# Layer 1 of a two-layer state-space kernel: 128 + 64 channels against three groups of 64 channels with two states per unit

## The chip, the core and the metric

The kernel runs on one core of a Trainium2 chip. A core has five engines that run side by side, each with its own instruction queue: TensorE (PE: matrix products into PSUM, with its weight loads shown apart as PEld), VectorE (DVE), ScalarE (ACT), GpSimd (POOL) and SyncE (SP, which here issues most DMAs). The metric is the device time of the whole kernel in microseconds, taken as the median of several runs; a profile gives one execution in detail, with the time of every instruction and the clock that TensorE was granted.

## What is computed

The input is a 64 x 64 picture with 96 channels (4096 tokens). Two layers follow one another, each with group norm ahead and a residual around it. Layer 0 is a scan in four directions, and the change does not touch it. Layer 1 is one forward scan over all 4096 tokens (192 inner channels, 16 states):

```python
xz = jnp.einsum('blc,ec->ble', u, W_in)
xs, z = jnp.split(xz, 2, axis=-1)
xc = silu(causal_conv(xs, conv_w, 3 taps) + conv_b)
dbc = jnp.einsum('bld,ed->ble', xc, W_x)          # dt (6), B (16), C (16)
delta = jax.nn.softplus(dt @ W_dt + b_dt)
dA = jnp.exp(delta[..., None] * A)
dBu = delta[..., None] * Bm[:, :, None, :] * xc[..., None]
h = dA_t * h + dBu_t                              # token after token
y = jnp.einsum('bdn,bn->bd', h, C_t)
out = ((y + xc * D) * silu(z)) @ W_out
```

All data are float32, except that B is split into three bfloat16 parts that add up to it, and is spread by a bfloat16 product.

## The kernel before

Layer 1 (class `Layer1`, line 709) works in 4 chunks of 1024 tokens (`CH`). In a chunk there are 24 *units*. A unit is one scan of a tile of 128 partitions x 1024 tokens, and its operations are spread over all engines:

- `load` (L895): a DMA brings the unit's rows of C from DRAM, each row repeated over partitions.
- `spread` (L909): PE multiplies a selection matrix `pick` with the split B (`parts`), two matmuls of 512 tokens, so that B of the unit's states stands in every partition of a PSUM tile `f`.
- `decay` (L901): ACT makes `dA` = exp(A dt).
- `scan` (L920): DVE multiplies `f` in place with `w` = dt u, and then scans `h` = dA h + f. The `f` pool has two buffers.
- `keep_last` (L929): ACT keeps the last column of `h` as the carry-in of the same unit in the next chunk.
- `times_c` (L933): POOL multiplies `C` in place with `h`.
- `fold` (L937): PE adds the result to `y` in PSUM.

The 192 channels are cut in 128 + 64. The first 16 units are the 16 states of the first 128 channels. In the last 8 units the two halves of the partitions hold two states of the other 64 channels, and `fold` adds the halves with a matrix `both` of 64 columns: the first 512 tokens go to partitions 0 to 63 of `y1`, the second 512 to partitions 64 to 127. A float32 matmul is recorded as two instructions, called *records* below; a bfloat16 one as one.

All front tiles (`u`, `sz`, `e`, `dt`, `w`) have 128 partitions x 1536 columns: 1024 columns for the 1024 tokens of the first 128 channels, and 512 columns whose partition halves are the two token halves of the other 64 channels. For the last 8 units this packed part of `dt` and `w` is copied by eight DMAs of 128 KB into `dt1` and `w1` (end of `front_dt`, L853), where both halves of the partitions hold all 1024 tokens. The first 16 units read `dt` and `w` themselves.

The order of each engine's instructions in layer 1 is the program's order (class `Ordered`). `run` (L1014) goes through all units; at step s it issues load(s+3), spread(s+1), keep_last(s-1), decay(s+2), scan(s), times_c(s-1), fold(s-2), and then one piece of `between` (L1000): the front of the next chunk and the back of the one before, cut by `yield` into pieces. The pieces are, in order: xn on ACT, three convolutions `pc` (`front_u`), in chunks 1 to 3 the back (`gate` of y1, and two pieces with the output product `po`), three products `pz` (`front_z`), silu on ACT with the first `pd`, the second `pd` with the DMA of C to DRAM (`front_dbl`), three `pv` (`front_v`), four pieces of softplus (exp, then `q` on ACT and `acc` on DVE, `front_dt`), one with the end of softplus and the copies, and two that split B (`front_b`). Products of these pieces share one PSUM buffer `misc`. For chunk 0 the front is run ahead of the first unit, in the order u, silu, dbl, b, v, dt, z.

`load_layer1` (L149) brings the weights at the very start of the program by seven DMAs on SP; the DMAs of x on SP stand behind them.

## Time and profile before

| what | us |
|---|---|
| median of 3 runs | 815.01 (811.65 to 816.62) |
| the profiled execution | 810.95 |
| its span, first to last instruction | 808.8 |
| layer 1: from its first xn to its first scan product | 300.3 to 355.25 |
| the four chunks (first product to first product) | 107.4, 116.5, 113.8, 90.0 |
| from the last scan's end to the end | 25.85 |
| busy over the span: PE, DVE, ACT, POOL | 633.6, 532.6, 325.2, 282.9 |
| mean granted TensorE clock | 0.808 |

Read it so: an engine's busy time says how much of the span it worked, and not that it set the end; "idle before" names what an engine waited for ahead of a group of instructions. The chunks are the part to look at, since each runs the same 24 units with a different amount of front and back work among them. DMA shares are means over 16 engines.

### The profile page before, as it was taken

Reading aid. Unit: us, or ns where it says so; the run is one execution under the profiler, and the core shown is the slowest. Engines: PE = TensorE matmul, PEld = TensorE weight load, DVE = VectorE, ACT = ScalarE, POOL = GpSimd, SP = SyncE. Lnnn points to the kernel's source line nnn. Section 1 sums busy time; section 2 is a strip of 40 time slices with the busy share of each in tenths; the row PEclk is TensorE's granted clock in tenths of the full one; section 3 lists DMA queues with packets and bytes.
Section 4 is the critical chain, followed back from the end, with each engine's and each line's share of the span. In section 5 each row is a group of like instructions: output and inputs, shape, how many; then the busy total and the mean of one; then the engine's idle time right before and its main releaser. Section 6 shows DMA issues by size and latency. Waiting matters only on the chain.

```text
span 808.8 us, 4869 instructions
## 1 busy us (share of the span) xinstructions
PE 633.6 (78%) x1497; PEld 238.4 (29%) x1497; DVE 532.6 (66%) x439; ACT 325.2 (40%) x458; POOL 282.9 (35%) x163
## 2 busy tenths in 40 slices
PE   1599999799999968549866699865699854796576
PEld 1344444343222222113221135321145320252115
DVE  2500359714975650188679977679987779989970
ACT  1211694513432222654663523664433662433200
POOL 9000000000000000206447954535954555856550
PEclk9699999989755586559888789896599985799955
DMA  6200170000000010046334723252634333554500
GB/s 150 78 1 0 57 199 0 0 1 19 0 10 10 21 38 0 3 114 198 100 111 110 201 105 118 83 159 54 193 118 140 115 106 96 191 152 152 148 9 24
DMA packets 29461, 68.49 MB, mean 85 GB/s; under 512 B 13008, under 2 KB 13420, under 8 KB 28978
## 3 DMA queue, kind: packets, MB, share of 16 engines
q1 hardware_dynamic: 26874, 65.91, 28.0%
q10 hardware_dynamic: 2552, 2.18, 1.0%
q8 instruction: 14, 0.23, 0.1%
q14 instruction: 21, 0.17, 0.1%
HBM read 60.36 MB, written 3.56 MB: 79 GB/s over the span
## 4 chain that ended last, share of the span: by engine, by line
PE 48%; DVE 28%; ACT 13%; issue 5%; DMA 2%; POOL 2%; SPq 1%; DVEq 0%; POOLq 0%; ACTq 0%
DVE h L695 13%; PE y L695 10%; PE pc L544 8%; PE po L695 5%; DVE f L695 4%; PE pc L695 4%; DVE acc L695 3%; PE pd L695 3%; PE f L695 3%; ACT dA L695 3%; PE pe L527 2%; DMA xt<-in_x 2%; PE pq L185 1%; PE pv L695 1%; PE pq L184 1%
## 5 line engine op out<-in xcount | busy, mean ns | idle before, releaser
L695 POOL TENSOR_TENSOR C<-C,h 128x1024 f32<-128x1024 f32 x96 | 234.9, 2453 | 177.7 <-DVE h L695 127.9
L695 DVE TENSOR_TENSOR_SCAN h<-dA,last,f 128x1024 f32<-128x1024 f32 x72 | 169.0, 2347 | 9.3
L695 DVE TENSOR_TENSOR f<-f,w 128x1024 f32<-128x1024 f32 x96 | 116.7, 1216 | 35.7 <-PE f L695 35.6
L695 PE MATMUL y<-C,ident 128*128 128x512 f32 x256 | 134.3, 648 | 0.1
L695 PE MATMUL f<-parts,pick 96*128 96x512 bf16 x192 | 69.9, 453 | 80.3 <-DVE h L695 79.8
L544 PE MATMUL pc<-pad,cw 96*128 96x512 f32 x288 | 127.2, 602 | 0.0
L695 ACT ACTIVATE dA<-dt,A 128x1024 f32<-128x1024 f32 x96 | 109.6, 1147 | 37.9 <-DVE h L695 37.4
L544 PEld LDWEIGHTS pc<-pad,cw 96*128 96x128 f32 x288 | 55.1, 192 | 70.6 <-issue 70.3
L695 PEld LDWEIGHTS y<-C,ident 128*128 128x128 f32 x256 | 53.4, 209 | 48.6 <-issue 39.1
L695 PE MATMUL y<-C,both 128*64 128x512 f32 x128 | 51.7, 902 | 16.5 <-POOL C L695 16.4
L695 PEld LDWEIGHTS <-pick 96*128 96x128 bf16 x192 | 14.0, 103 | 166.6 <-DVE h L695 126.7
L695 DVE TENSOR_TENSOR_SCAN h<-dA,f 128x1024 f32<-128x1024 f32 x24 | 54.9, 2287 | 2.9
L555 DVE TENSOR_SCALAR u<-u,d 128x512 f32<-128x512 f32 x16 | 8.3, 523 | 73.1 <-ACT u L550 73.0
L695 POOL MEMSET xn<- 96x2 f32 x1 | 0.1, 97 | 149.5 <-PE po L185 149.5
L695 PE MATMUL pc<-xn,cw 96*128 96x512 f32 (+1 forms) x96 | 38.7, 663 | 2.9 <-ACT xn L695 2.9
L695 DVE SCALAR_TENSOR_TENSOR acc<-q,e 128x1536 f32<-128x1536 f32 x4 | 7.0, 1758 | 51.0 <-ACT q L695 51.0
L695 ACT COPY last<-h 128x1 f32<-128x1 f32 x72 | 13.6, 189 | 61.2 <-DVE h L695 61.1
L654 DVE RECIPROCAL sd<-sd 128x512 f32<-128x512 f32 x8 | 26.7, 3345 | 10.1 <-ACT sd L653 10.1
L695 PE MATMUL pd<-u,w_x 128*118 128x512 f32 (+1 forms) x32 | 23.6, 850 | 10.7 <-ACT u L695 10.7
L550 ACT ACTIVATE u<-pc,vec 128x512 f32<-128x512 f32 x16 | 10.8, 685 | 50.7 <-PE pc L544 50.6
L695 ACT COPY ob<-po 128x384 f32<-128x384 f32 x8 | 3.8, 478 | 67.8 <-PE po L695 67.8
L695 PE MATMUL po<-w_out,v 64*128 64x96 f32 (+1 forms) x128 | 29.1, 331 | 0.7 <-ACT ob L695 0.6
(157 smaller groups left out, 730.3 us busy)
## 6 DMA issues: line engine op xcount, KB each, us to landing
C<-c_dram SPq DMA_DIRECT2D x64, 512.0 KB, 3.7
C<-c_dram SPq DMA_DIRECT2D x64, 256.0 KB, 3.6
dt<-dt SPq DMA_DIRECT2D x16, 128.0 KB, 2.3
w<-w SPq DMA_DIRECT2D x16, 128.0 KB, 2.3
xT_dram<-xT SPq DMA_DIRECT2D x1, 1536.0 KB
xc<-xT_dram SPq DMA_DIRECT2D x8, 192.0 KB, 2.5
out<-ob SPq DMA_DIRECT2D x8, 192.0 KB, 2.2
wB<-rows_dram SPq DMA_DIRECT2D x1, 1472.0 KB
```

Source lines behind the costliest of these rows:

```text
L184: nc.tensor.matmul(out, w[0], rhs0, start=True, stop=False)
L185: nc.tensor.matmul(out, w[1], rhs1, start=False, stop=True)
L527: nc.tensor.matmul(pe, cw[:, j, t * P : (t + 1) * P], free(pad, (W - side, 2), (W + 2, H), (1, side), at=j // 3 * (W + 2) + j % 3), start= ...
L544: nc.tensor.matmul(pc, cw[:, j, t * P : (t + 1) * P], pad[:, c * rows + j // 3 : (c + 1) * rows + j // 3, j % 3 : j % 3 + W], start=(j == ...
L550: nc.scalar.activation(u, pc, AF.Silu, bias=lay["vec"][:, CB + t : CB + t + 1])
L555: nc.vector.tensor_scalar(v[:, t, col], u, k["d4"][:, t : t + 1], None, ALU.mult)
L654: nc.vector.reciprocal(sd, sd)
L695: ins = it(*args, **kw)
```

## The change

Layer 1's 192 channels are cut in three groups of 64. Every unit now holds two states (j and j + 8) of one group in the two halves of the partitions; unit i of a chunk is state pair i // 3 of group i % 3. There are still 24 units in a chunk, with the same tiles of 128 x 1024.

- One `spread` and one `load` serve a state pair, that is, three units: B stands in its own PSUM tile (one buffer), C in its own tile (three buffers). The spread of the next pair is issued at the third unit of a pair, behind its fold and ahead of its piece.
- DVE's product reads `B` and writes a PSUM tile `f` of one buffer. POOL writes a new tile `p` instead of overwriting C.
- Every fold is of the half-width kind, into three tiles `y0`, `y1`, `y2`.
- All front tiles are packed: 3 x 512 columns, the partition halves being token halves (`by_group` for `both_tiles`). `pd` takes three products of 64 rows a half for one of 128 and one of 64.
- All of `dt` and `w` is copied by DMA into `dts` and `ws` (128 x 3 x 1024), eight DMAs of 64 x 3 x 512 a chunk, and every unit reads the copies.
- `back` is cut into four pieces and its output product has four terms for three; the gates are three of 512 columns, issued at the first three steps of the next chunk. `front_b` is run beside `front_v`, ahead of softplus. In the front of chunk 0, v comes ahead of b, xn is made by DVE in two halves, and three PSUM buffers take turns.
- `dA` has three buffers instead of four. `load_layer1` has sixteen DMAs on SP (six of them of 64 x 3 single numbers, six of 64 x 8).

The core of the diff:

```diff
-                ("fix", 1), ("xn", 1), ("uz", 2), ("sp", 1), ("dt", 2), ("dup", 2), ("dbl", 1),
-                ("parts", 2), ("split", 1), ("C", 6), ("dA", 4), ("h", 3), ("v", 1), ("ob", 2),
+                ("fix", 1), ("xn", 1), ("u", 2), ("sz", 2), ("sp", 1), ("dt", 1), ("dup", 2),
+                ("dbl", 1), ("parts", 2), ("split", 1), ("C", 3), ("dA", 3), ("h", 3), ("p", 3),
+                ("ob", 2),
...
-        for n, b, width in (("f", 2, CH), ("y0", 1, CH), ("y1", 1, NB), ("misc", 1, NB)):
+        for n, width in (("B", CH), ("f", CH), ("misc", NB), *((f"y{i}", NB) for i in range(NG))):
...
+    def by_group(self, c, name, taps, evict):
+        for g in range(NG):
+            ps = self.misc([P, NB], f"{name}{g}", c)
+            for j, (w, x) in enumerate(taps):
+                for hf in range(2):
+                    self.nc.tensor.matmul(
+                        ps[self.half(hf), :], w[:, g * HALF : (g + 1) * HALF],
+                        x[:, self.tokens(hf)], start=(j == 0), stop=(j == len(taps) - 1),
+                    )
+            evict(g, slice(g * NB, (g + 1) * NB), ps)
+            yield
...
+        for key, src in (("dts", dt), ("ws", w)):
+            of[key] = both = self.tile("dup", [P, NG, CH], key, c)
             for share in range(2):
                 for hf in range(2):
                     nc.sync.dma_start(
-                        to[self.half1(share), hf * NB : hf * NB + NB], src[self.half1(hf), CH:CW]
+                        both[self.half(share), :, self.tokens(hf)],
+                        src[self.half(hf), :].rearrange("p (g s) -> p g s", g=NG),
                     )
...
+    def spread(self, pair):
+        c, j = divmod(pair, NJ)
+        self.B[pair] = b = self.tile("B", [P, CH], "B", pair)
+        for hf in range(2):
+            self.nc.tensor.matmul(
+                b[:, self.tokens(hf)], self.k["pick"][:, j, :],
+                self.chunks[c]["B"][:, self.tokens(hf)], start=True, stop=True,
+            )
...
     def scan(self, s):
+        of, (c, i), g = self.units[s], divmod(s, UNIT), s % NG
+        f = self.tile("f", [P, CH], "f", s)
-        self.nc.vector.tensor_mul(of["f"], of["f"], self.chunks[c]["w"][i // NS])
+        self.nc.vector.tensor_mul(f, self.B[s // NG], self.chunks[c]["ws"][:, g, :])
...
+        of["p"] = self.tile("p", [P, CH], "p", s)
+        self.nc.gpsimd.tensor_mul(of["p"], self.C[s // NG], of["h"])
...
+        for hf in range(2):
+            nc.tensor.matmul(
+                chunk[f"y{g}"][self.half(hf), :], k["fold"][1][:, 0:HALF],
+                of["p"][:, self.tokens(hf)], start=False, stop=(i >= UNIT - NG),
+            )
...
             yield from self.front_dbl(c + 1, after)
-            yield from self.front_v(c + 1, after)
+            b = self.front_b(c + 1, after)
+            for _ in self.front_v(c + 1, after):
+                next(b, None)
+                yield
             yield from self.front_dt(c + 1, after)
-            yield from self.front_b(c + 1, after)
...
-            if s + 1 < n:
-                self.spread(s + 1)
+            if g == 0 and s // NG + 2 < n // NG:
+                self.load(s // NG + 2)
...
+            if g == NG - 1 and s + 1 < n:
+                self.spread(s // NG + 1)
+            if s >= UNIT and i < NG:
+                self.gate(c - 1, g)
```

## The prediction

> **What bounds the kernel now.** First the table of stages (busy time of each engine between the first scan product of each chunk). Columns: stretch, length, then PE, weight loads, DVE, ACT, POOL, granted clock, DMA share, GB/s.

> ```profile
> 300.30:355.25 54.95, 32.38 (x52) 9.26 (x52) 10.54 (x6) 26.55 (x28) 4.23 (x2) 0.56 0.02 4
> 355.25:462.66 107.41, 80.57 (x188) 26.30 (x188) 91.88 (x54) 56.13 (x76) 65.59 (x26) 0.82 0.54 153
> 462.66:579.12 116.46, 89.85 (x242) 33.73 (x242) 95.64 (x56) 55.15 (x77) 63.83 (x26) 0.80 0.39 118
> 579.12:692.96 113.84, 89.63 (x246) 33.52 (x246) 95.46 (x57) 55.14 (x77) 66.60 (x28) 0.81 0.42 125
> 692.96:782.95 89.99, 66.80 (x204) 25.61 (x204) 85.22 (x51) 25.78 (x25) 59.24 (x26) 0.92 0.43 129
> 782.95:808.80 25.85, 17.27 (x54) 11.84 (x52) 0.69 (x1) 0.96 (x2) 2.34 (x1) 0.50 0.07 20
> ```

> Rows 2 to 5 are the four chunks, 427.7 us together; DVE works in 368.2 of them. The last chunk, with no front for a next one, is almost pure DVE; in the two middle ones DVE idles 20 us each. The groups of instructions say for whom.

> ```profile
> L695 DVE TENSOR_TENSOR f<-f,w 128x1024 f32<-128x1024 f32 x96 | 116.7, 1216 | 35.7 <-PE f L695 35.6
> L695 PE MATMUL y<-C,ident 128*128 128x512 f32 x256 | 134.3, 648 | 0.1
> L695 PE MATMUL f<-parts,pick 96*128 96x512 bf16 x192 | 69.9, 453 | 80.3 <-DVE h L695 79.8
> L695 PE MATMUL y<-C,both 128*64 128x512 f32 x128 | 51.7, 902 | 16.5 <-POOL C L695 16.4
> L695 DVE SCALAR_TENSOR_TENSOR acc<-q,e 128x1536 f32<-128x1536 f32 x4 | 7.0, 1758 | 51.0 <-ACT q L695 51.0
> ```

> So DVE waits 35.6 us for the spread of B, and 11.7 us in the chunks (39.3 of the 51.0 lie before the first scan) for the first q of softplus. A pair of half-width folds runs side by side: 51.7/128 = 0.40 us a record against 134.3/256 = 0.52, though one alone is longer (902 ns).

> A steady unit, in the timeline (start, length):

> ```profile
> 452.04 1.21 DVE L695 TENSOR_TENSOR f<-f,w 128x1024 f32<-128x1024 f32 x1
> 453.38 2.29 DVE L695 TENSOR_TENSOR_SCAN h<-dA,f 128x1024 f32<-128x1024 f32 x1
> 455.58 1.21 DVE L695 TENSOR_TENSOR f<-f,w 128x1024 f32<-128x1024 f32 x1
> 456.92 2.29 DVE L695 TENSOR_TENSOR_SCAN h<-dA,f 128x1024 f32<-128x1024 f32 x1
> ```

> The unit is 3.54 us (452.04 to 455.58), 3.61 with a carry-in. Where the scan reads the product, 0.13 us lie between them (452.04+1.21 to 453.38). The next product, in the other f buffer, starts 0.09 us before the scan has ended.

> **Gain: TensorE.** 16 of a chunk's 24 folds become half-width pairs, 4 x 16 x 4 records x (0.52-0.40) = 31 us of PE; spreads fall from 192 to 64 records, 128 x 0.36 = 46 us. DVE's floor for the chunks is 24 units x 3.54 (then 3.61), three times four acc and a dt (8.5), and four chunks' gates (2.0 each, the last but one on the chunk after): 85+8.5, twice 97.1, 88.6, or 376 us. Against 427.7, 52 us could go. I take these back one by one.

> **Cost 1: product and scan share one f.** f had two PSUM buffers; now one, and every product carries a wait for the scan before it. Nothing shows this pair, and a wait more can only cost; nearest are the 0.13 us gap of a dependent pair and the 0.09 us overlap of an independent one: 0.22 us a unit, bounds 0 and 0.22. I take 0.22. It counts where a product follows a scan directly and no longer wait covers it: chunk 0: 7 units before silu, 6 after dt; middle chunks 8 and 2 each; last 21. That is 54 x 0.22 = 12 us. [...]

> **Cost 2: the copies.** Each group needs dt and w for both token halves on both partition halves, so all of dt and w is copied: 8 x 64 x 3 x 2 KB = 3.15 MB a chunk, where 1.05 MB were copied for tile 1 only, long before use. The old copies after the first softplus run alone here:

> ```profile
> 355.00:356.00 1.00, 0.00 (x0) 0.00 (x0) 0.87 (x2) 1.00 (x2) 0.00 (x0) 0.50 0.89 201
> 356.00:357.00 1.00, 0.00 (x0) 0.00 (x0) 0.90 (x2) 1.00 (x2) 0.00 (x0) 0.50 1.01 217
> 357.00:358.00 1.00, 0.00 (x0) 0.00 (x0) 1.00 (x1) 0.72 (x1) 0.00 (x0) 0.50 0.90 199
> 358.00:359.00 1.00, 0.07 (x1) 0.07 (x2) 1.00 (x2) 0.09 (x1) 0.00 (x0) 0.50 0.93 201
> ```

> The last two columns are the DMA share and GB/s. About 205 GB/s at a nearly full share: 15.3 us for 3.15 MB. Bounds: 9.2 (the C loads' 340 GB/s) and 18. At the start the first product stood 1.9 us after dt; now it stands 1.1 (issue to data) + 15.3 + 0.5 (landing) = 17 us after: **+15.1** (9 to 18). Between chunks 1, 2 and 3 the front ends at step 20: dt is ready 1.7 us after scan 20 and the copies 1.1+15.3+0.6 later, at 18.7. The next chunk's first product is wanted after three more units, at 1.7 + 3 x 3.61 + 2 x 0.22 = 13.0: a wait of **5.7** at the starts of chunks 2 and 3 (bounds 0 and 8). Chunk 1 has its dt four units earlier and waits for nothing. Behind the copies on SP stand the C loads of the next pairs, two pairs ahead of use: covered. On POOL times_c queues behind the 3.42 us w product and catches up 1.1 us a unit: covered. [...]

> **Cost 3: ACT before the first acc.** In chunk 1 ACT took from 510.54 to 539.62, 29.1 us, from the silu step to the first acc: 20.5 us of own work, 8.6 of waits for pd and pv. DVE needs 6 units, 21.7. The change puts front_b's three casts (3.1 us) in that stretch and makes both pd longer (6 records for 4, 0.5 to 0.99 us each): +5 to +7. It takes out most of the 8.6 us of waits, in which PE worked on full folds and spreads ahead of pd and pv: -4 to -8. I leave 29.1; bounds 25 and 32. So the 7.4 us stall stays, three times.

> **Cost 4: PE's remaining lag.** The spread waits for the third product of a pair, behind the work of the step before. At 0.43 us a record pc is 2.6, po 2.7 a step (32 records a half instead of 24), a fold pair 0.9. Steps 1 to 7 of a middle chunk hold 27.2 us of PE against 27.3 of DVE, so DVE waits little: 1 us in chunk 0, 2 in the middle ones, 1.5 in the last. At half clock it would be some 5 to 6 more a chunk; the bounds are 0 and 25 together. It cannot be a gain: it is counted from DVE's floor.

> **Start, end and load.** pd at the start: 12 records for 8 at 0.5 to 0.99 us: +1.4 to +3.9, I take 2.6; v before b on ACT: +0.5 to +2.1, I take 1.3; xn on DVE in two halves (0.54 each) for 1.24 on ACT: -0.4. With the copies the stretch before the first product is 18.6 us longer. At the end po has four terms for three: the 64-row term took 0.67 us with its loads (timeline, 790.00 to 790.67), the identity term 0.38; 0.6 for the one more, four times in each of two halves, **+4.8** (2.4 to 6). The 16 layer-1 DMAs for 7 on SP ahead of x (0.55 us each) delay its issue 4.6 us, but ACT's own x and conv weights, which shared the DMA engines from 9 to 16 us, then go first; **+0.5** (0 to 5). One diag more, and a POOL pick fewer, are hidden by group norm and by the x load.

> **The sum.** Chunk 0: 7 x 3.76 + 1 + 29.1 + 11 x 3.54 + 8.5 + 1.3 = 106.1. Chunks 1 and 2: 11 x 3.61 + 1.8 + 2.0 + 2 + 29.1 + 7 x 3.61 + 8.5 + 0.4 + 5.7 = 114.5 each. Chunk 3: 24 x 3.61 + 2.0 + 4.6 + 1.5 = 94.7. Together 429.8, 2.1 more than before: what PE gives back is spent on the copies' wait, the f wait and a stall that stays. 2.1 + 18.6 + 4.8 + 0.5 = +26.0. The profiled execution took 810.95 us (span 808.8, 2.15 around it): **837 us**. The median of the runs, 815.01, is 0.5% above that execution; the forecast for a median might be 4 us more.

> **Rivals.** (a) *Copies off the path* (not slower): the place is the first product and the two chunk starts. Without them 837 - 15.1 - 11.4 = 810. It decides for "no change" once 3.15 MB take under 7.4 us (425 GB/s): 837 - 7.9 - 11.4 = 818. Against it: no SBUF to SBUF stretch above 217. Chance 0.10. (b) *f wait free*: DVE overlaps product and scan as now, 837 - 12 = 825. For it: same engine, in order. 0.18. (c) *PE at half clock becomes the bound*. PE's busy time and clock in two steady stretches:

> ```profile
> 560.00:580.00 20.00, 10.16 (x22) 0.50 0.56 157
> 740.00:760.00 20.00, 12.57 (x33) 1.00 0.48 136
> ```

> Fewer matmuls mean more like the first. pd 6 records then take 5.9, fold pairs 2.0, and each chunk loses 5 to 6: 837 + 22 = 859. Against it: the second line, and PE is busy without a break in steps 1 to 7. 0.14. (d) *ACT's stretch shrinks to its own work*, 20.5 + 3.1 of casts, so that it ends 5 us earlier in three chunks: 837 - 15 = 822. For it: PE has less ahead of pd and pv; against it: misc still has one buffer. 0.10. (e) What a, b and d price all cheap at once, 837 - 27 - 12 - 15 = 783, or two of the three, to 798: 0.06. My forecast, all four costs: 0.42.

> **How the numbers follow.** A measurement of this kernel tells about 1% from no change. Faster by over 1% is (e): 0.06. Within 1%: (a), and 0.03 of (d) and (b) together: 0.13. Slower: the forecast, c, and the rest of b and d: 0.81. The range runs from 812 (a, with x not delayed) to 860 (c); the forecast's own is 826 to 848.

> **What would show it.** In the profile after: f product to product in a steady unit 3.76 or 3.54; first product 17 us after dt's end; DVE waiting for DMA at two chunk starts, some 5 us each; acc waiting for q some 7 us, three times; DVE's wait for PE under 10 us, not 35.6; the tail near 31. Wrong would be above all: copies at over 300 GB/s, or long waits of the product for B.

## The result, and the profile after

The changed kernel takes **862.08 us** (median of 4 runs, 858.67 to 864.82) against 813.33 us for the kernel before in the same comparison: ratio 1.0595, 95% interval 1.0537 to 1.0654. The forecast was 837 us, the range 812 to 860. Here and below, a median is over all runs of a kernel, while a ratio and its interval leave out slow runs, more than 1.5% above the fastest of their kernel (two of the four in run 8). The profiled execution took 862.2 us, its span is 860.5; against the span of before, 808.8, that is +51.7 where +26 was forecast.

The table of stages again: from the first normalised column of layer 1 to the first scan product, then the four chunks, then the tail.

```profile
304.54:372.01 67.47, 30.14 (x82) 11.96 (x84) 11.54 (x9) 27.52 (x29) 4.23 (x2) 0.60 0.26 53
372.01:486.30 114.29, 76.92 (x180) 15.77 (x176) 92.38 (x53) 53.99 (x74) 65.64 (x26) 0.62 0.31 71
486.30:608.91 122.61, 90.41 (x272) 25.56 (x270) 96.48 (x57) 57.57 (x80) 70.36 (x28) 0.67 0.26 62
608.91:733.12 124.21, 85.12 (x242) 23.86 (x242) 96.47 (x56) 54.11 (x76) 68.00 (x27) 0.66 0.27 63
733.12:831.87 98.75, 67.07 (x176) 21.92 (x176) 87.36 (x52) 24.66 (x23) 54.06 (x23) 0.59 0.14 38
831.87:860.50 28.63, 20.37 (x70) 15.12 (x68) 1.96 (x3) 0.96 (x2) 2.35 (x1) 0.50 0.07 18
```

The first product stands 16.8 us later than before (372.01 against 355.25), the tail is 2.8 longer, and the chunks take 459.9 us against 427.7: +32.2, where the forecast had +2.1. DVE is busy for as long as before in them (372.7 against 368.2); it is its waits that grew. And PE's granted clock in the chunks is 0.59 to 0.67, where it was 0.80 to 0.92. The groups and the waits of DVE say for whom it waits (the numbers of a wait are its sum, how often, the longest):

```profile
L698 PE MATMUL y<-p,both 128*64 128x512 f32 x384 | 159.2, 923 | 90.7 <-POOL p L698 90.2
L698 DVE TENSOR_TENSOR f<-B,ws 128x1024 f32<-128x1024 f32 x96 | 118.1, 1230 | 75.4 <-PE B L698 42.8
L698 PE MATMUL pd<-u,w_x 64*118 64x512 f32 x48 | 38.3, 1031 | 11.3 <-ACT u L698 11.3
```

```profile
DVE acc L698 <- ACT q L698: 55.1, 7, 34.8
DVE f L698 <- PE B L698: 42.8, 8, 8.4
DVE f L698 <- DMA ws<-w: 29.6, 3, 16.1
```

The 29.6 us for the copies are the ones forecast (16.1 at the start, 6.65 and 6.80 at the starts of chunks 2 and 3). The 42.8 us for the spread of B are new. They begin where PE's timeline looks like this, in chunk 1:

```profile
534.47 5.47 PE L698 MATMUL pd<-u,w_x 64*118 64x512 f32 x6 [1.79 <-ACT u L698]
539.87 1.98 PE L698 MATMUL y<-p,both 128*64 128x512 f32 x4
541.77 5.47 PE L698 MATMUL pd<-u,w_x 64*118 64x512 f32 x6
547.17 1.97 PE L698 MATMUL y<-p,both 128*64 128x512 f32 x4
549.07 1.97 PE L698 MATMUL pv<-dbl,dtw 6*64 6x512 f32 x4
...
552.88 1.03 PE L698 MATMUL B<-parts,pick 96*128 96x512 bf16 x2
```

PE works without a break, but six records of pd take 5.47 us (0.91 us each; the shortest pd record of the trace is 0.59), a pair of folds 1.97 (1.08 at 506.46, where the granted clock is 1.00). The third product of the pair is over long before the spread at 552.88 can come; the next product then starts at 553.95, after 8.4 us of idle DVE. ACT meanwhile waits for the same pd and pv. From the start of the silu of u to the first acc it takes 36.2, 34.3 and 34.3 us in chunks 0 to 2, where it took 26.5, 26.5 and 24.8; of that stretch, its waits for PE are 13.7, 13.1 and 13.1 us, where they were 7.2, 8.6 and 6.9. That is 9.8, 7.8 and 9.5 us more, 27 together, beside the 30.1 us that the chunks lost against the forecast.

### The profile page after: what moved, and what is told of

It is laid out like the page before. It is cut to its first block, busy times and chain, and to the rows that moved or that the text cites. A ratio compares the mean times of both kernels' runs of the same rounds, so it can differ in the third digit from the quotient of the medians.

```text
span 860.5 us, 4838 instructions
## 1 busy us (share of the span) xinstructions
PE 626.6 (73%) x1529; PEld 212.1 (25%) x1529; DVE 537.2 (62%) x446; ACT 324.3 (38%) x457; POOL 279.7 (33%) x154
## 4 chain that ended last, share of the span: by engine, by line
DVE 24%; PE 16%; issue 7%; ACT 5%; DMA 4%; POOL 4%; SPq 2%; DVEq 0%; POOLq 0%; ACTq 0%
DVE h L698 14%; DVE f L698 7%; PE po L698 6%; PE y L698 5%; POOL p L698 3%; PE pc L698 3%; DMA ws<-w 3%; DVE acc L698 3%; SPq L698 2%; ACT dA L698 1%; ACT q L698 1%; ACT e L698 1%; DMA C<-c_dram 1%; PE B L698 1%; PE pv L698 1%
## 5 line engine op out<-in xcount | busy, mean ns | idle before, releaser
L698 POOL TENSOR_TENSOR p<-C,h 128x1024 f32<-128x1024 f32 x96 | 237.7, 2481 | 182.4 <-DVE h L698 179.5
L698 PE MATMUL y<-p,both 128*64 128x512 f32 x384 | 159.2, 923 | 90.7 <-POOL p L698 90.2
L698 DVE TENSOR_TENSOR f<-B,ws 128x1024 f32<-128x1024 f32 x96 | 118.1, 1230 | 75.4 <-PE B L698 42.8
L698 ACT ACTIVATE dA<-dts,A 128x1024 f32<-128x1024 f32 x96 | 109.6, 1147 | 77.6 <-DVE h L698 52.8
L698 PEld LDWEIGHTS y<-p,both 128*64 128x64 f32 x384 | 25.8, 182 | 199.3 <-POOL p L698 172.2
L698 PE MATMUL B<-parts,pick 96*128 96x512 bf16 x64 | 29.6, 559 | 47.2 <-DVE f L698 30.2
L698 PE MATMUL pc<-xn,cw 96*64 96x512 f32 x144 | 45.3, 778 | 18.7 <-ACT xn L698 16.6
L698 PE MATMUL pd<-u,w_x 64*118 64x512 f32 x48 | 38.3, 1031 | 11.3 <-ACT u L698 11.3
L698 PE MATMUL po<-w_out,sz 64*128 64x96 f32 x192 | 38.6, 351 | 0.6 <-ACT ob L698 0.6
L698 PEld LDWEIGHTS po<-w_out,sz 64*128 64x128 f32 x192 | 32.3, 246 | 15.4 <-issue 8.9
L698 ACT ACTIVATE q<-e,quad 128x1536 f32<-128x1536 f32 x16 | 25.2, 1575 | 12.8 <-DVE acc L698 12.4
```

Of the source, the lines that this page charges most:

```text
L698: ins = it(*args, **kw)
```

## The experiments

All take the changed kernel (862 us) and edit it, but for one. Each comparison had its own runs of the kernel before; their medians lie between 807.5 and 811.6. The end of the first dt, up to which nearly all of them have the same code, lies between 347 and 362 us in the profiles, so stages are compared, not only totals.

The theories: **A**, one B buffer that is free only after the third product, with its spread behind other work in PE's order; **B**, PE's low clock and load, whatever the order; later **C**, the clock follows the rows that the products fill; **D**, front_b's casts lie in ACT's chain.

**1. Two B buffers, f moved to SBUF.**

```diff
-        f = self.tile("f", [P, CH], "f", s)
+        of["h"] = f = self.tile("h", [P, CH], "h", s)
...
-            if g == NG - 1 and s + 1 < n:
+            if g == 0 and s // NG + 1 < n // NG:
                 self.spread(s // NG + 1)
```

> B gets two PSUM buffers, and the spread of the next pair is issued two units earlier (at the first unit of a pair, not at the last). The room comes from f, which goes to SBUF: the product writes the buffer of h and the scan works in it in place. Theory A (the single B sits in PE's order behind front and back work that itself waits for ACT): the 42.8 us for which the product waits for B go down to under 8, and with three h buffers the f wait goes too (0.14 us a unit, about 9): 862 - 35 - 9 = 818 us, 812 to 828. Rival B (the half clock of PE is the cause, whatever the order): PE is as late as before, its wait only moves to the folds and from there to POOL and h; product waits stay above 25 us, 845 to 855 us.

**2. f in SBUF alone.** The first hunk of the diff above, without the second buffer.

> Only f moves: into the three buffers of h in SBUF, scan in place; B single and the order as in the changed kernel. If the wait of the product for the scan before it costs what 3.54 against 3.68 us a unit says, some 65 units gain 0.14 us: 862 - 9 = 853 us, unit 3.54, and the waits for B stay at 42.8 or grow by part of the gain. Theory A: no more than that, 850 to 858. Rival (f with one buffer is what bounds the chunks): below 840.

**3. The same with three constant products a step.**

```diff
+                for _ in range(3):
+                    self.nc.tensor.matmul(
+                        self.idle, self.k["pick"][:, 0, :], self.k["pick"][:, 0:4, :], start=True, stop=True
+                    )
```

> As the run with f in SBUF and B single, with three bf16 products of constants (128 x 512, into a PSUM bank that nobody reads) added at the end of every step, behind the work of that step: they add about 0.7 to 0.8 us of PE a unit and are to keep the granted clock up. Rival B (the clock alone): clock from 0.70 to over 0.85, pd six records from 5.5 to under 3.5 us, waits for B down by half or more, 830 to 840 us. Theory A (order and the chain through ACT): the waits for B fall by at most a third, 845 to 855. If the added work is itself late: above 862.

Measured: 907.5, 913.6 and 923.6 us, all worse than the changed kernel, for a reason that neither theory had. The wait for B was gone in the first, but the mean carry-in scan went from 2.35 to 3.19 us (3.31 in the second). DVE's and POOL's timeline of the second show why:

```profile
453.93 2.29 DVE L698 TENSOR_TENSOR_SCAN h<-dA,h 128x1024 f32<-128x1024 f32 x1
...
459.04 3.19 DVE L698 TENSOR_TENSOR_SCAN h<-dA,h 128x1024 f32<-128x1024 f32 x1
...
456.39 3.69 POOL L698 TENSOR_TENSOR p<-C,h 128x1024 f32<-128x1024 f32 x1 [5.25 <-DVE h L698]
```

In these rows the scan takes 2.29 us with POOL idle, and 3.19 with POOL's product beside it. POOL's product started while DVE's acc ran until 457.87, and took 3.69 instead of 2.35; the scan that began at 459.04 took about as long as if it had made headway only once POOL had ended at 460.08 (460.08 + 2.29 = 462.37, its end was 462.23). So f stays in PSUM from here on; by the means above, 96 scans x some 0.85 us are the price of moving it (an estimate). The clock was not raised far by the third kernel (0.73 against 0.67), and the test of A had to be made otherwise.

**4. Two B buffers, f in PSUM.** The banks come from y: the three groups are added into one, so that this kernel leaves out keeping their sums apart.

```diff
-        for n, width in (("B", CH), ("f", CH), ("misc", NB), *((f"y{i}", NB) for i in range(NG))):
+        for n, b in (("B", 2), ("f", 1), ("misc", 1), ("y", 1)):
...
-            if g == NG - 1 and s + 1 < n:
+            if g == 0 and s // NG + 1 < n // NG:
```

> B gets two PSUM buffers, and its spread is issued two units earlier, while f stays in PSUM with one buffer. The two banks come from y: the three groups are added into one bank, so that the output is not the reference's; the three gates stand together at the second unit of the next chunk. Records and bytes are as in the changed kernel. Theory A: waits for B from 42.8 to under 5, f wait as it was: 862 - 38 = 824 us, 818 to 832. From the run with f in SBUF, where the waits for B went to zero with a second buffer, I hold this far likelier than rival B (855 to 865). If the scan stays at 2.35 us beside POOL, the 3.2 us of the runs with f in SBUF are the price of SBUF for both of its inputs.

Measured: 855.4 us, where theory A had 818 to 832 (ratio to before 1.0571, 1.0442 to 1.07: not told apart from the changed kernel's 1.0595). This is the run that felled theory A. No wait for B is left (the 6.7 us put down to pc are the wait for the copies at the start of chunk 2):

```profile
L698 DVE TENSOR_TENSOR f<-B,ws 128x1024 f32<-128x1024 f32 x96 | 118.2, 1231 | 33.4 <-DMA ws<-w 22.7 <-PE pc L698 6.7
```

and yet chunks 0 to 2 take 112.3, 122.3 and 122.6 us against 114.3, 122.6 and 124.2. The waits came back elsewhere: the scan now waits 16.3 us for POOL (whose products stand behind rest, which waits for ACT's cast) and 9.6 for ACT's dA, and acc 8 us instead of 6 for q. The stretch from silu to acc is still 35.3 to 36.2 us: it sets these chunks, and a product that waits less for B only waits more for something else. Only the last chunk, which has no front, gained (98.8 to 92.0).

**5. A spread of B per unit, as before the change.**

```diff
-        f = self.tile("f", [P, CH], "f", s)
-        self.nc.vector.tensor_mul(f, self.B[s // NG], self.chunks[c]["ws"][:, g, :])
+        f = of["f"]
+        self.nc.vector.tensor_mul(f, f, self.chunks[c]["ws"][:, g, :])
```

> Undoes one part: B no longer serves three units. Each unit has its own spread again, into one of two PSUM buffers of f, with the product in place, as in the kernel before; C, the groups and the copies stay as changed. Theory A (one B buffer that is only free after the third product, behind other PE work): a spread now needs only the scan two units back, so a late PE has a unit more of slack; waits of the product for PE 42.8 down to some 20, the f wait of 0.14 us a unit gone too (9): 862 - 23 - 9 = 830 us, 820 to 840. Rival B (PE's load at half clock is the cause, not the order): 128 records more of 0.36 to 0.5 us are 46 to 64 us of PE; the waits stay or grow: 855 to 875 us.

**6. No front or back work ahead of the spread.**

```diff
-                next(work, None)
+                for _ in range((1, 0, 2)[g]):
+                    next(work, None)
```

> Order alone: of front and back work, which is issued a piece a unit, no piece is issued at the middle unit of a pair and two at the last, behind the spread. So nothing of front or back stands ahead of the spread in PE's order but the fold. Theory A: the waits of the product for B fall from 42.8 to 10 to 20; some come back as longer bursts of work ahead of the folds: 862 - 25 = 837 us, 830 to 848. Rival B (clock and load, whatever the order): waits above 35 us, 855 to 868 us.

Measured: 855.4 us for the first (ratio 1.0591, 1.0449 to 1.0734), what theory B had put it at, though its waits for PE did not grow (36.2 us): all of what the chunks gained lies in the last chunk (88.4 us for 98.8), as in run 4. The second took 892.8 us, worse than either theory had it: the waits for B stayed (48.2 us), and two pieces in one step made the carry-in scans wait 16.4 us for dA and POOL, where they had waited 0.5.

**7. More work for PE, to raise the clock.**

```diff
+                for _ in range(3 if NG + 1 < i < UNIT - NG else 0):
+                    self.nc.tensor.matmul(
+                        self.chunks[c]["y0"], self.k["zero"], self.k["pick"][:, 0:4, :],
+                        start=False, stop=False,
+                    )
```

> Clock alone: behind the work of each step (units 5 to 20 of each chunk) three bf16 products with zero weights, 128 x 512, are added into the y of group 0, which they leave as it is. All buffers and the order stay. They add 0.7 to 1.3 us of PE a unit. Rival B: the granted clock rises from 0.70 to 0.8 or more, pd six records from 5.5 to 3.5 us or less, waits for B fall to under 25: 840 to 848 us. Theory A: what PE gains in clock it pays in records, the waits for B stay above 35: 858 to 870 us.

Measured: 866.5 us. The mean clock rose from 0.704 to 0.742, but not where it was needed: the median pd record stayed at 1.054 us. Three products of 96 x 128 a step were not enough to raise it there.

**8. Full rows.** pd and po take all 128 rows and pv 102, the rows of others with zero weights.

```diff
-                    ps, lay["w_x"][self.half(hf), g, :], u[self.half(hf), g * NB : (g + 1) * NB],
+                    ps, lay["w_x"][:, hf, g, :], u[:, g * NB : (g + 1) * NB],
...
-        rows = slice(DT_ROW, DT_ROW + R)
+        rows = slice(0, DT_ROW + R)
...
-                    (v[half, g * NB + j * P : g * NB + (j + 1) * P], lay["w_out"][half, g, :])
+                    (v[:, g * NB + j * P : g * NB + (j + 1) * P], lay["w_out"][:, hf, g, :])
```

> The products of 64 and of 6 rows are given full rows: pd and po take all 128 rows and pv 102, with zero weights for the rows that are not theirs. Records, their order and their results are the same. In the changed kernel PE was busy for 17 to 20 us of 20 at a clock of 0.50 where pd and pv run (410 to 430, 660 to 680), and at 0.92 where the 96-row pc runs (490 to 520). Theory C (the clock follows how much of the array the products fill, not how busy PE is): pd six records from 5.5 to 3 to 3.5 us, the stretch from silu to the first acc 5 to 8 us shorter, three times: 862 - 20 = 842 us, 835 to 850. Rival (the clock follows something else): pd stays at 5.5 us, 858 to 866 us.

Measured: **830.4 us** (818.5 to 838.2; ratio to before 1.0232, 1.0117 to 1.0348), 32 us less by the medians, more than the 842 expected, with not one record fewer. The records of a tile in the changed kernel (shortest/median/longest, in ns):

```profile
L698 PE MATMUL pd<-u,w_x x48: 589/1057/1202, 319.6 to 670.3; 64*118 64x512 f32 x48
L698 PE MATMUL pv<-dbl,dtw x48: 587/1056/1111, 325.0 to 684.7; 6*64 6x512 f32 x48
```

and with full rows:

```profile
L703 PE MATMUL pd<-u,w_x x48: 591/688/1204, 322.8 to 659.3; 128*118 128x512 f32 x48
L703 PE MATMUL pv<-dbl,dtw x48: 590/594/1116, 330.6 to 671.2; 102*64 102x512 f32 x48
```

The same stretch of chunk 1 as above, now:

```profile
534.74 5.13 PE L703 MATMUL pd<-u,w_x 128*118 128x512 f32 x6 [2.21 <-ACT u L703]
539.80 1.08 PE L703 MATMUL y<-p,both 128*64 128x512 f32 x4
540.81 2.83 PE L703 MATMUL pd<-u,w_x 128*118 128x512 f32 x6
543.57 1.08 PE L703 MATMUL y<-p,both 128*64 128x512 f32 x4
544.48 1.03 PE L703 MATMUL pv<-dbl,dtw 102*64 102x512 f32 x4
```

The first pd still runs slowly, and from then on everything takes half as long: the folds too, though nothing was done to them. From silu to acc it is 30.0, 28.3 and 28.1 us, the waits for B sink from 42.8 to 15.4, and the chunks from 459.9 to 433.1.

**9. Full rows for pd alone:** the first hunk of run 8 without the other two.

> The changed kernel with full rows for pd alone (pv at 6 and po at 64 rows as changed). If each product's own rows raise the clock: pd records from 1.06 us in the median to about 0.7, pv stays near 1.0: 862 - 15 = 847 us, 842 to 853, about half of the gain of all three (830). Rival (the mix over a longer time counts, and pd alone is too little): pd above 0.95 us, 856 to 865.

Measured: 837.3 us, three quarters of the gain. pv, at 6 rows as in the changed kernel, has a median of 0.638 us instead of 1.056: so it isn't its own rows alone that slow it; of PE's products only pd, ahead of it, had been changed. That part of the expectation was wrong, and 837.3 us lies below its range.

**10. front_b behind front_dt again.**

```diff
-            b = self.front_b(c + 1, after)
-            for _ in self.front_v(c + 1, after):
-                next(b, None)
-                yield
+            yield from self.front_v(c + 1, after)
             yield from self.front_dt(c + 1, after)
+            yield from self.front_b(c + 1, after)
```

> Undoes one part: front_b (three casts on ACT, two differences on POOL) again stands behind front_dt, not beside front_v. Theory D (the casts, and POOL's products behind the wait for them, lie in the stretch from silu to the first acc): the stretch gets 3 to 5 us shorter, three times, and POOL's wait of 14 us ahead of rest goes: 862 - 12 = 850 us, 845 to 855. Rival (PE's pieces set that stretch, the casts lie in its waits): 858 to 866 us, the waits of acc for q as before.

Measured: 848.7 us (ratio 1.0534, 1.0466 to 1.0602); silu to acc 33.1, 32.2 and 32.2 us, 3.1, 2.1 and 2.1 less, where the three casts had stood (3.1 us), and the chunks 451.4 us for 459.9. Theory D holds in kind; in two of the three chunks the stretch shrank by less than the 3 to 5 us expected.

**11. The copies in order of groups.**

```diff
-                    nc.sync.dma_start(
-                        both[self.half(share), :, self.tokens(hf)],
-                        src[self.half(hf), :].rearrange("p (g s) -> p g s", g=NG),
-                    )
+                        nc.sync.dma_start(
+                            of[key][self.half(share), g, self.tokens(hf)],
+                            src[self.half(hf), g * NB : (g + 1) * NB],
+                        )
```

(with the loop over the groups outermost)

> The 3.15 MB of copies of dt and w in 24 DMAs ordered by group (dt and w of group 0 first) instead of 8 ordered by array. Nothing else changes. If the bytes ahead of the first product cost the time: the first product stands 1.1 + 15.3/3 + about 2 = 8 to 9 us after dt instead of 17.9 (-9), and of the 6.7 us waits at two chunk starts some 4 each go: 862 - 17 = 845 us, 840 to 850. Rival: 24 issues at 0.55 us on one queue (13 us) set the rate, and the C loads behind them come late: 855 to 865.

Measured: 840.8 us (833.6 to 850.6). The first product stands 7.0 us after dt instead of 17.9, and the waits at the starts of chunks 2 and 3 are gone. Chunk 0 took 5.4 us longer, as its first C loads now stand behind 24 copies (POOL waited 36.5 us for C).

**12 and 13. The sums,** runs 8 and 11 together, with B shared and with a spread per unit. Both also move the first C loads ahead of the copies and the layer-1 loads behind x:

```diff
+            if step == self.front_dbl:
+                self.load(0)
+                self.load(1)
...
-    lay1 = load_layer1(nc, const, vec1, w_z1, w_x1, dt_w1, w_out1)
+    lay1 = {}
+    k["later"] = lambda: lay1.update(load_layer1(nc, const, vec1, w_z1, w_x1, dt_w1, w_out1))
```

> What each cost is said to be, taken out together, with B still serving three units: copies by group (measured 841 alone), the first two C loads of the kernel ahead of the copies (the changed kernel's POOL did not wait for them, the run by group did, 36 us), the layer-1 loads behind x (-4 at the start), full rows for pd, pv and po. If theory C holds: 841 - 4 - 4 - 15 = 818 us, 808 to 828. If the rows do nothing: 833, 826 to 838.

> As the run before this one, with a spread of B per unit again (two f buffers, product in place). Alone that gained 7 us (862 to 855), in the last chunk only (98.8 to 88.4); in the others the waits of the product for PE stayed. If PE at half clock made them, they go now: 818 - 12 = 806 us, 798 to 815, below the kernel before. If the stretch from silu to acc through ACT and the single misc buffer sets the chunk: no more than the last chunk's gain, 810 to 828.

**14 and 15. The same two with front_b late.**

> The sum of before (copies by group, first C loads ahead of them, layer-1 loads behind x, full rows; 805 us) with front_b behind front_dt again. Alone that gained 13 us, 10 of them in the two middle chunks; with full rows the stretch from silu to acc is shorter already, but POOL's product still waits there behind rest (4.4 us in chunk 0): 805 - 6 = 799 us, 793 to 805. Rival (full rows have taken the same time already): 803 to 808 us.

> The same with a spread of B per unit (two f buffers). Where B still waited (12.8 us in chunk 0, 5.2 in chunk 2 of the sum) it does so because its spread stands behind a fold that waits for POOL; front_b late takes that away for both forms: 799 us, 792 to 805, within 4 us of the run before this one. Rival (the shared B has a price of its own): this one is 6 us or more below the other.

**16. The kernel before with full rows.**

```diff
-            nc.tensor.matmul(ps, lay["w_x"][1][half, :], u[half, CH:CW], start=False, stop=True)
+            nc.tensor.matmul(ps, lay["w_x"][1][:, hf, :], u[:, CH:CW], start=False, stop=True)
...
-        rows = slice(DT_ROW, DT_ROW + R)
+        rows = slice(0, DT_ROW + R)
...
-                    (v[half, CH + j * P : CH + (j + 1) * P], lay["w_out"][1][half, :]),
+                    (v[:, CH + j * P : CH + (j + 1) * P], lay["w_out"][1][:, hf, :]),
```

> The kernel before with full rows for its products of 64 and 6 rows (tile 1 of pd and po, all of pv), by zero weights. Its pd records are 0.75 us in the median, its pv 0.64, against 0.59 at full clock; ACT's waits for pd and pv were 8.6 us between silu and the first acc in chunk 1. If the clock follows the rows there too, half of that goes, in three chunks, and some of the 35.6 us of the product's wait: 811 - 12 = 799 us, 792 to 806. Rival (half of its pd has full rows already, the clock is up anyway): 807 to 813 us.

Measured, for runs 12 to 16 in order: 805.5 and 805.2 us, then 800.3 (ratio 0.9875, 0.983 to 0.9919) and 797.1 (0.9851, 0.9803 to 0.9899), and **782.6 us** for the kernel before with full rows (0.9664, 0.9614 to 0.9714). So the layout of the change can beat the kernel before, by 1.2 and 1.5%, once its costs are mended; but the kernel before gains 29 us by the full rows alone, and stays ahead. The narrow products were thus a price that both kernels paid: with full rows in both, the chunks still stand 24.7 us apart (433.1 against 408.4), where they stood 32.2 apart. Most of what the change loses there comes from the other costs, which the remaining runs took away: the copies' order, front_b's place, and the one buffer of f. Stages, in us:

| kernel | dt to first product | chunks 0 to 3 | sum | tail |
|---|---|---|---|---|
| before | 1.9 | 107.4, 116.5, 113.8, 90.0 | 427.7 | 25.9 |
| changed | 17.9 | 114.3, 122.6, 124.2, 98.8 | 459.9 | 28.6 |
| full rows | 17.9 | 110.4, 114.2, 116.6, 92.0 | 433.1 | 25.4 |
| sum, front_b late | 6.9 | 114.2, 105.6, 106.0, 91.7 | 417.6 | 25.9 |
| the same, spread per unit | 6.9 | 109.8, 107.3, 105.9, 88.4 | 411.4 | 25.7 |
| before, full rows | 1.9 | 103.7, 107.1, 109.1, 88.3 | 408.4 | 22.7 |

Run 15 against run 16 is what is left of the change with the cures in both: the start 5 us, the tail 3, the chunks 3, and 2.5 ahead of them. Runs 14 and 15 came where they were expected (800.3 and 797.1 us for 799), run 12 beyond its range (805.5 for 818), and the gain of run 16 was more than twice the one expected (29 us for 12). Run 13 met its 806 us by luck: it was to gain 12 us over run 12, and gained 0.3. Whether the shared B has a price of its own in the total is not shown (3 us between runs 14 and 15, whose runs overlap). In the last chunk it is 3.3 us (91.7 against 88.4), and there it is the price of f's one buffer: units of 3.74 us (742.77 to 746.52 us in run 14) against 3.60 (742.60 to 746.20 in run 15), 24 times.

## Why the prediction was right or wrong

- **Gain: TensorE.** Right in records, not in time. The folds take 159.2 us instead of 186.0 (-27 for -31 forecast), the spreads 29.6 instead of 69.9 (-40 for -46); yet PE is busy for 626.6 us instead of 633.6, as front and back came in more records (48 of pd for 32, 38.3 us for 23.6) and everything ran at a mean clock of 0.704 instead of 0.808. The last chunk, which has neither pd nor pv, shows the change's own part in that clock: 0.59 for 0.92 (0.63 with full rows, run 8).
- **Cost 1.** Right in kind, too large: products of chunk 0 start at 383.06, 386.74 and 390.43, 3.68 and 3.69 us apart, later 3.74 (502.66 to 506.40): 0.13 to 0.15 more than 3.54 and 3.61, not 0.22.
- **Cost 2.** Right: +16.0 before the first product for 15.1, and 6.65 and 6.80 us at two chunk starts for 5.7.
- **Cost 3 is the step that failed.** It left ACT's stretch as it was, as PE would have less ahead of pd and pv and the waits for them would shrink by 4 to 8 us. They grew by 4.5 to 6.5 instead (in chunk 1 from 8.6 to 13.1), because pd and pv themselves came to run at half clock (0.50 from 532.56 to 552.88, below), and the casts added 3.1. The stretch got 7.8 to 9.8 us longer, where the bound allowed 2.9 (32 against 29.1). Runs 8 and 10 took 6 us and 2 to 3 us of it away.
- **Cost 4** was sized at 6.5 us; the product waited 42.8 us for B. The text named the half clock and priced it (5 to 6 a chunk, rival c at 859 us), but held it unlikely since PE would be busy without a break in steps 1 to 7. So it was, and there the clock was 0.92 (490 to 520, PE busy for all 30 us). In chunk 1 it fell behind these steps, at 529.15, when PE had been busy for 1.57 of 3.41 us, 5 us ahead of the first pd. Under pd and pv it stayed at 0.50 with PE busy again, for 18.53 of 20.32 us; the last row is the same place in chunk 2:

```profile
505.26:525.74 20.48, 20.36 (x106) 10.70 (x106) 18.14 (x11) 9.49 (x17) 11.81 (x5) 1.00 0.16 46
525.74:529.15 3.41, 1.57 (x10) 0.30 (x6) 3.24 (x3) 1.84 (x4) 2.35 (x1) 1.00 0.54 154
532.56:552.88 20.32, 18.53 (x29) 4.64 (x29) 12.27 (x7) 9.84 (x13) 4.98 (x3) 0.50 0.12 29
660.00:680.00 20.00, 19.89 (x33) 4.27 (x31) 10.98 (x7) 8.23 (x13) 5.58 (x4) 0.50 0.13 30
```

- **Rival c** came within 3 us of the result, in part by luck. Its pieces were right (six pd records 5.47 us for 5.9, a fold pair 1.97 for 2.0), and so was its reason in the last chunk. Where pd and pv run it was another: PE is busy there for 18.53 of 20.32 us at 0.50 (above), and full rows in these products brought the mean clock of chunks 1 and 2 from 0.67 and 0.66 to 0.74 and 0.73 (run 8). And it priced 22 us where the chunks missed by 30, which the start and the tail made up in part.
- **Start, end and load.** The tail grew by 2.8 us, not 4.8. PE began 4.3 us later on x, but the first dt came 0.8 us later, since the front of chunk 0 took 49.6 us from xn instead of 53.0, where 3.5 more were forecast. Why it is shorter wasn't tried.
- Against the forecast of +26.0 the chunks missed by +30.1, the start by -2.3 and the tail by -2.0: together 25.8 of the 51.7 us. One term of the sum was added wrongly: chunk 0 comes to 105.2 us and not 106.1, and the forecast by its own terms to 836.

Busy time as the trace counts it did not bring the full clock back: the last row above has 19.89 busy us of 20 at 0.50, and run 8 raised the clock of chunks 1 and 2 with PE busy for less time in them (77.87 and 72.05 us instead of 90.41 and 85.12).

## What to carry to other kernels

Ask of a change that splits a product into narrower ones what clock PE will have afterwards, not only how many records it saves: here zero weights in the unused rows of 64-row and 6-row products took 32 us off the changed kernel and 29 off the kernel before, with no record more. A wait that an engine shows is not yet the bound: taking all 42.8 us of it away (run 4) moved the median by 7 us, nearly all of it in the last chunk: in the others the chain through ACT set the chunk, and the wait came back under another name. And try a cure on the kernel before as well; the best version here is the old layout with full rows.

## What the runs showed of the hardware

- PE had a granted clock of 0.50 while busy for 19.89 of 20 us (660 to 680 in the changed kernel), with products of 64 and 6 rows and folds of 64 columns between them. With zero weights in the other rows the median pd record took 0.688 us instead of 1.057 (run 8) and, in the kernel before, 0.592 instead of 0.752 (run 16). In the fit above, an estimate from the eighteen profiles, streaming time times the share of rows and of columns in a window of 3.41 us tells the clock of the next one by a border of 1.27 us, in all but 20 of 2851.
- In run 2, where both inputs of the scan lay in SBUF, the scan took 3.19 us beside POOL's product and 2.29 with POOL idle, and POOL's product took 3.69 when it started under DVE's acc, against 2.35 in the changed kernel (at 510.26). There, with f in PSUM, the carry-in scan takes 2.35 us on the mean, with POOL at work as well.
- A product that waits by semaphore for the scan just ahead of it on DVE made a unit of 3.68 us in the changed kernel (383.06 to 386.74), one that writes another buffer 3.54 in the kernel before (452.04 to 455.58): 0.14 us.
